# Loads of the experts' results moved into both arms of a branch, and the unused products in front of the last sums taken out

## The chip, the cores and the metric

The kernel runs on one core of one Trainium2 chip. Its time is device microseconds for one execution. The time before is 732.98 us, the median of 3 runs (732.32 to 736.02). All durations of single instructions below come from one profiled execution, which took 734.5 us.

## The reference

Two transformer layers on x of 2048 tokens by 128 features, fp32. After each of four sublayers the result is added to its input and normalised over the features (mean and variance, no gain). The first two are an attention with 16 heads and a Fourier filter; the third is a linear attention with 8 heads. The fourth is what matters here: a mixture of 8 experts, of which every token uses two.

```python
probs = softmax(flat @ router_w)                 # 2048 x 8
topw, topi = top_k(probs, 2)
combine = sum(one_hot(topi, 8) * topw[..., None], axis=1)
h = silu(einsum('td,edf->tef', flat, w1) + b1)   # 512 hidden features
y = einsum('tef,efd->ted', h, w2) + b2
out = einsum('te,ted->td', combine, y)
x = layernorm(x + res + out)                     # the last norm: the output
```

## The kernel before, in words

The tokens lie in 16 tiles of 128 rows; four tiles make a block, and there are NB = 4 blocks. The three earlier sublayers and the router take the first 625 us of the span and are not touched.

The experts work on sorted rows. The router's stage writes each token's row twice, once for each of its two experts, into the DRAM buffer `xr`, sorted by expert. A loop over pieces of BK = 256 rows then runs the experts (`experts`, L1472): `fetch_rows` loads a piece of `xr` on SyncE's queue, `copy_weights` picks the weights of its expert, `turn_rows`, `first` and `second` are the products on TensorE, and `back` (L1449) turns the piece back, scales it by the router's weight and scatters its rows by two indirect DMAs of GpSimd (L1458) into the DRAM buffer `yr`, where the first 2048 rows are the tokens' first choices and the other 2048 their second choices.

How many pieces there are depends on the data: 23 (NBK) at most. The first 19 (OFTEN) are always run. The last four are under a branch, `tc.If(many > OFTEN)` (L1504), which every engine takes for itself from a register. With the inputs used here 19 pieces suffice: the profile has 19 fetches and 38 scatters, so the other arm is the one that runs. It has no code of the kernel in it. It has only what the framework puts there: instructions that wait for the work before the branch and raise each semaphore by what the arm with four pieces would have added, so that both arms leave the same counts. The framework gives every hardware DMA one of eight semaphores in rotation, and every scatter one of eight others.

Behind the branch (L1507 to L1567) the output is made. For each block `b`:

- two loads of 256 KB fetch the first and second choices' results, `yk[0]` on SyncE's queue and `yk[1]` on ScalarE's (L1521). They read all of `yr`, so they wait for the last scatter.
- `add(b, x4s, ...)` (L1524) multiplies the residual `x4s` by the identity into the PSUM tile `zs[b]`. The 128x512 fp32 product runs as two matmul instructions.
- `sum_up(b)` (L1531) adds both `yk` to the same PSUM tile in the same way, four instructions a block.
- `stats_of` (L1535, with `stats` at L1052) has VectorE take mean and variance, `root_of` has GpSimd take the root, `shift_of` and `put` have ScalarE (for the last block VectorE too) write the normalised rows, and SyncE stores them (L1555).

Between the four residual products and the first `sum_up` stand five products of the identity with `x4s` into a tile `warm` that nothing reads (L1526 to L1529; ten instructions). From `sum_up` on, each engine keeps the order in which the kernel's text has it (`held`, L1567).

Of the kernel before, what the change touches and what calls it, by code (L numbers as in the profile page):

```python
# [9 lines left out]
F32 = mybir.dt.float32  # L10
# [8 lines left out]
P = 128  # L19
# [8 lines left out]
def tile_postln_stack(ctx: ExitStack, tc: tile.TileContext, a: dict, out: bass.AP):  # L28
    nc = tc.nc
    T, D = a["x"].shape  # L30
    NT = T // P
    TB = 4
    BW = TB * P
    NB = NT // TB
# [9 lines left out]
    NBK = 2 * T // BK + E - 1  # L44
# [13 lines left out]
    ident = const.tile([P, P], F32, name="ident")  # L58
# [77 lines left out]
    def bc(v):  # L136
        return v.unsqueeze(1).to_broadcast([P, TB, D])
# [5 lines left out]
    def slot(name):  # L143
        return banks[2].tile([P, 2, BW], F32, tag="slot", name=name)
# [18 lines left out]
    with ExitStack() as l0:  # L163
# [13 lines left out]
        warm = slot("warm")  # L177
# [405 lines left out]
        for k in range(NQ):  # L583
            b = k // 2
# [9 lines left out]
            for t in range(QT):  # L594
                i = k * QT + t
                for c in range(NP):
# [12 lines left out]
                    for heads_of, g, nt in groups:  # L609
# [3 lines left out]
                        for n, j in enumerate(heads_of):  # L613
                            for mask in (False, True)[: 1 + (g == NG - 1)]:
                                for half in range(2):
# [4 lines left out]
                                    if mask:  # L620
# [4 lines left out]
                                            start=False,  # L625
                                            stop=True,
                                        )
                                    else:
# [4 lines left out]
                                            start=True,  # L633
                                            stop=(g < NG - 1),
# [402 lines left out]
    for e in range(0, E, 2):  # L1037
        nc.sync.dma_start(
            out=wall[:, e : e + 2],
            in_=a["we"].rearrange("(e p) c -> p e c", p=P)[:, e : e + 2],  # L1040
# [8 lines left out]
    ps_a = ctx.enter_context(tc.tile_pool(name="ps_a", bufs=4, space=PSUM))  # L1049
    la = ctx.enter_context(tc.tile_pool(name="l1a", bufs=1))  # L1050
    lm = ctx.enter_context(tc.tile_pool(name="l1m", bufs=3))
# [12 lines left out]
    x4s = la.tile([P, NT, D], F32, name="x4s")  # L1064
# [261 lines left out]
    for step in SEQUENCE.split():  # L1326
        name, of = step.split(":")
# [7 lines left out]
    warm = ps.tile([P, BW], F32, tag="p", name="warm")  # L1335
    for _ in range(15):
# [4 lines left out]
            start=True,  # L1341
            stop=True,
# [30 lines left out]
    def registers(n, engine, top):  # L1373
# [10 lines left out]
    many = nc.values_load(  # L1384
        used[0:1, :],
        min_val=0,
        max_val=NBK,
        skip_runtime_bounds_check_because="so many blocks at most",
    )

    def fetch_rows(j):
        xb = lm.tile([P, KT, ROW], F32, name="xb", bufs=SOON + 2)
        nc.sync.dma_start(
            out=xb, in_=xr[bass.ds(firsts[j], BK), :].rearrange("(t p) c -> p t c", p=P)
        )
        xbs[j] = xb
# [3 lines left out]
    def copy_weights(j):  # L1400
        wt = lm.tile([P, WC], F32, name="wt", bufs=AHEAD)
        nc.vector.tensor_copy(wt, flat[:, bass.ds(offsets[j], WC)])
        wts[j] = wt

    def turn_rows(j):
        xb = xbs[j]
        pt = ps.tile([P, KT, P], F32, tag="p", name="px5")
        for t in range(KT):
            nc.tensor.transpose(pt[:, t, :], xb[:, t, 0:D], ident)
        xT = lm.tile([P, BK], F32, name="xT5")  # L1410
        nc.vector.tensor_scalar(  # L1411
            xT,
            pt.rearrange("p t d -> p (t d)"),
            cols[:, 2:3],
            cols[:, 3:4],
            ALU.mult,
            ALU.add,
        )
        xTs1[j] = xT

    def first(j):
        wt, xT = wts[j], xTs1.pop(j)
        hu = lm.tile([P, NF, BK], F32, name="hu", bufs=2)
        for f in range(0, NF, 2):
            pu = ps_a.tile([P, 2, BK], F32, tag="acc", name="pu")
            for n in range(2):
                nc.tensor.matmul(pu[:, n], wt[:, ts(f + n, P)], xT, start=True, stop=True)  # L1427
                nc.scalar.activation(  # L1428
                    hu[:, f + n],
                    pu[:, n],  # L1430
                    AF.Silu,
                    bias=wt[:, 2 * NF * P + f + n : 2 * NF * P + f + n + 1],
                )
        hus[j] = hu

    def second(j):
        wt, hu = wts.pop(j), hus.pop(j)
        acc = ps_a.tile([P, BK], F32, tag="acc", name="acc")
        for f in range(NF):
            nc.tensor.matmul(  # L1440
                acc, wt[:, ts(NF + f, P)], hu[:, f], start=(f == 0), stop=(f == NF - 1)
            )
        yT = lm.tile([P, KT, P], F32, name="yT5")
        nc.vector.tensor_scalar(
            yT.rearrange("p t d -> p (t d)"), acc, wt[:, WC - 1 : WC], None, ALU.add
        )
        yTs[j] = yT

    def back(j):  # L1449
        xb, yT = xbs.pop(j), yTs.pop(j)  # L1450
        pt = ps.tile([P, KT, P], F32, tag="p", name="py5")
        for t in range(KT):
            nc.tensor.transpose(pt[:, t, :], yT[:, t, :], ident)
        yb = lm.tile([P, KT, D], F32, name="yb")
        for t in range(KT):
            nc.vector.tensor_scalar_mul(yb[:, t], pt[:, t], xb[:, t, D + 1 : D + 2])  # L1456
        for t in range(KT):
            put = nc.gpsimd.indirect_dma_start(  # L1458
                out=yr[:, :],
                out_offset=bass.IndirectOffsetOnAxis(  # L1460
                    ap=xb.bitcast(U32)[:, t, D : D + 1], axis=0
                ),
                in_=yb[:, t, :],
                in_offset=None,
                bounds_check=2 * T - 1,
                oob_is_err=False,
            )
            tc.declare_no_dep(put.ins, group="back", reason="every row is written once")
            tc.add_to_no_dep_group("back", put.ins)
        return put  # L1470

    def experts(begin, end):  # L1472

        put = None
        for j in range(begin, min(begin + AHEAD - 1, end)):
            copy_weights(j)
        for j in range(begin, min(begin + SOON, end)):
            fetch_rows(j)
        turn_rows(begin)
        for j in range(begin, end):  # L1480
            if j + SOON < end:
                fetch_rows(j + SOON)
            first(j)
            if j + 1 < end:
                turn_rows(j + 1)
            if j > begin:
                put = back(j - 1)
            second(j)
            if j + AHEAD - 1 < end:
                copy_weights(j + AHEAD - 1)  # L1490
            if 4 <= j < 4 + NB:
                bt = ts(j - 4, TB)
                with tc.issue_after(put.ins):
                    nc.gpsimd.tensor_tensor(x3s[:, bt, :], x3s[:, bt, :], bc(mixc), ALU.subtract)
            if 4 + NB <= j < 4 + 2 * NB:
                bt = ts(j - 4 - NB, TB)
                with tc.issue_after(put.ins):
                    nc.gpsimd.tensor_tensor(x4s[:, bt, :], x3s[:, bt, :], x4s[:, bt, :], ALU.add)
        back(end - 1)


    OFTEN = NBK - E // 2
    experts(0, OFTEN)
    with tc.If(many > OFTEN, preferred_fallthrough_block=False):  # L1504
        experts(OFTEN, NBK)

    y_v = yr.rearrange("(k n p) d -> k p n d", k=2, p=P)  # L1507


    yks, zs, mvs, rs, nbs = {}, {}, {}, {}, {}  # L1510

    def add(b, src, start, stop):
        nc.tensor.matmul(  # L1513
            zs[b], ident, src.rearrange("p t d -> p (t d)"), start=start, stop=stop
        )

    for b in range(NB):
        bt = ts(b, TB)
        yk = [lm.tile([P, TB, D], F32, tag="mid", name=f"yk{k}", bufs=8) for k in range(2)]
        for k in range(2):  # L1520
            (nc.sync, nc.scalar)[k].dma_start(out=yk[k], in_=y_v[k, :, bt, :])  # L1521
        yks[b] = yk
        zs[b] = ps.tile([P, BW], F32, tag="p", name="z5")
        add(b, x4s[:, bt, :], True, False)  # L1524
    warm = ps_a.tile([P, BW], F32, tag="acc", name="warm2")
    for _ in range(5):  # L1526
        nc.tensor.matmul(  # L1527
            warm, ident, x4s[:, NT - TB :].rearrange("p t d -> p (t d)"), start=True, stop=True
        )  # L1529

    def sum_up(b):  # L1531
        for k in range(2):
            add(b, yks[b][k], False, k == 1)
# [96 lines left out]
```

## Time and profile before

| what | us |
|---|---|
| median of 3 runs | 732.98 |
| lowest, highest | 732.32, 736.02 |
| the profiled execution | 734.5 |
| its span, first to last instruction | 732.8 |
| first product of the experts (L1427) | 625.4 |
| last scatter issued (L1458) | 706.4 |
| loads of `yk` issued (L1521) | 710.6 to 712.2 |
| first statistics of the last norm (L1056) | 717.4 |
| last store issued (L1555) | 728.4 |

Of the span TensorE is busy 90%, VectorE 73%, ScalarE 64% and GpSimd 27%. These are averages over very different stages; the change is in the last 25 us. The rows of a profile name the source line, the engine, the operation and its tiles; an engine's name with a q is its sequencer, which issues DMAs and runs semaphore and branch instructions. Times are from the start of the span. The granted clock of TensorE (PEclk) is given as a share of full speed.

### The profile page before, as it was taken

What the parts mean: (1) busy time and instruction counts of PE and PEld (TensorE: products, weight loads), DVE (VectorE), ACT (ScalarE), POOL (GpSimd) and SP (SyncE); (2) the same over time, 40 slices, a digit from 0 to 9 for tenths busy, and PEclk for the clock granted to TensorE, in tenths of its full rate; (3) what the DMA queues carried; (4) which work ended last, traced back from release to release, by engine and by line L of the source; (5) the groups of instructions that cost most, each with busy time, mean ns of one, the idle gap of its engine ahead of it and who ended that gap; (6) DMA issues with size and microseconds to landing.
All of it is one profiled execution on the core that took longest, in us unless ns stands there. A gap on an engine that the chain in (4) does not pass through costs nothing. (4 is left out here: it accounts for less than half of the span.)

```text
span 732.8 us, 10664 instructions
## 1 busy us (share of the span) xinstructions
PE 660.5 (90%) x3745; PEld 374.9 (51%) x3745; DVE 531.6 (73%) x893; ACT 469.2 (64%) x1080; POOL 196.2 (27%) x203
## 2 busy tenths in 40 slices
PE   8999999999899988998899988899999818999984
PEld 7876555454345543433443333245567503788851
DVE  2566888887689897987799879887984654465514
ACT  2886988777788886876697778752554531344312
POOL 2412200220020220200500004030442786278532
PEclk9999999999999999999899999999999957999998
DMA  5802250220000214200069920050500011212115
GB/s 154 257 1 61 56 117 1 59 58 1 1 0 1 59 39 80 59 0 1 0 134 216 203 39 1 29 116 1 232 1 1 30 45 51 73 59 64 36 54 136
DMA packets 43622, 46.29 MB, mean 63 GB/s; under 512 B 3164, under 2 KB 33378, under 8 KB 43568
## 3 DMA queue, kind: packets, MB, share of 16 engines
q1 hardware_dynamic: 38896, 39.79, 23.9%
q0 software_dynamic: 2272, 4.24, 1.6%
q10 hardware_dynamic: 2400, 1.57, 0.9%
q8 instruction: 30, 0.49, 0.3%
q14 instruction: 24, 0.20, 0.1%
HBM read 23.13 MB, written 14.45 MB: 51 GB/s over the span
## 5 line engine op out<-in xcount | busy, mean ns | idle before, releaser
L647 ACT ACTIVATE sc<-sc,nmx 128x1024 f32<-128x1024 f32 (+7 forms) x384 | 321.6, 838 | 93.3 <-DVE nmx L644 65.8
L629 PE MATMUL sc<-kT,q 64*128 64x512 f32 (+7 forms) x1536 | 297.1, 508 | 19.0 <-ACT sc L647 18.0
L644 DVE TENSOR_REDUCE nmx<-sc 128x1 f32<-128x1024 f32 (+3 forms) x256 | 273.4, 1115 | 33.7 <-PE sc L629 19.6
L629 PEld LDWEIGHTS sc<-kT,q 64*128 64x128 f32 x1536 | 121.7, 187 | 143.0 <-ACT sc L647 86.8
L352 POOL TENSOR_TENSOR prod<-q,kT 128x1024 f32<-128x1024 f32 x16 | 37.5, 2350 | 195.5 <-PE pdl L364 68.0
L647 ACT ACTIVATION_READ_ACCUMULATOR sc<-sc,nmx 128x1 f32 x384 | 75.8, 197 | 0.0
L1428 ACT ACTIVATE hu<-pu,wt 128x256 f32<-128x256 f32 x76 | 33.4, 475 | 60.4 <-PE pu L1427 58.6
L104 POOL TENSOR_TENSOR ln_rs<-ln_rs,half_m 128x4 f32<-128x4 f32 x8 | 8.3, 1035 | 195.6 <-DVE ln_rs L103 195.6
L637 DVE TENSOR_REDUCE nmx<-sc 128x2 f32<-128x256 f32 (+3 forms) x64 | 51.7, 818 | 11.9 <-PE sc L621 11.3
L1458 POOL DMA_INDIRECT yr<-yb,xb x38 | 41.2, 1084 | 36.3 <-DVE yb L1456 29.3
L621 PE MATMUL sc<-rmask,lmask 64*128 64x64 bf16 x512 | 50.6, 189 | 0.0
L1427 PE MATMUL pu<-xT,wt 128*128 128x256 f32 x152 | 41.1, 393 | 0.4 <-DVE xT L1411 0.4
L621 PEld LDWEIGHTS <-lmask 64*128 64x128 bf16 x512 | 27.9, 102 | 20.8 <-issue 13.7
L1440 PE MATMUL acc<-hu,wt 128*128 128x256 f32 x152 | 35.9, 379 | 0.0
L1289 POOL DMA_INDIRECT xr<-rows,slots x32 | 31.6, 987 | 13.2 <-issue 7.9
L455 PE MATMUL pv<-x2T,pv 128*128 128x512 f32 x64 | 31.0, 612 | 2.5 <-DVE wx L461 2.1
L327 PE MATMUL pq<-x2T,pq 128*128 128x256 f32 x128 | 31.9, 392 | 1.4 <-ACT sc L647 0.9
L467 PE MATMUL py<-wx,po 128*128 128x512 f32 x64 | 31.0, 612 | 0.0
L1427 PEld LDWEIGHTS pu<-xT,wt 128*128 128x128 f32 x152 | 26.7, 189 | 8.0 <-ACT hu L1428 3.8
L1440 PEld LDWEIGHTS acc<-hu,wt 128*128 128x128 f32 x152 | 27.5, 190 | 3.2
L327 PEld LDWEIGHTS pq<-x2T,pq 128*128 128x128 f32 x128 | 23.2, 190 | 10.9 <-ACT sc L647 6.8
L461 DVE TENSOR_TENSOR wx<-pv,wx 128x1024 f32<-128x1024 f32 x16 | 19.4, 1222 | 11.4 <-DMA wx<-wd 5.9
(268 smaller groups left out, 785.4 us busy)
## 6 DMA issues: line engine op xcount, KB each, us to landing
xr<-pad SPq DMA_DIRECT2D x10, 845.0 KB, 15.4
q<-q SPq DMA_DIRECT2D x32, 256.0 KB, 3.7
wx<-wd SPq DMA_DIRECT2D x8, 1024.0 KB, 9.9
wall<-in_we_dram SPq DMA_DIRECT2D x4, 1029.0 KB, 9.5
xb<-xr SPq DMA_DIRECT2D x19, 130.0 KB, 2.3
x2T<-in_xT_dram SPq DMA_DIRECT2D x4, 256.0 KB, 5.1
xs<-in_x_dram SPq DMA_DIRECT2D x4, 256.0 KB, 6.8
yk<-yr SPq DMA_DIRECT2D x4, 256.0 KB, 5.8
```

The costliest lines, as they stand in the source:

```text
L327: nc.tensor.matmul(pm[:, n // 2, ts(n % 2, QW)], pq[:, ts(c + n, P)], x2T[:, ts(k, QW)], start=True, stop=True,)
L352: nc.gpsimd.tensor_tensor(prod, q.rearrange("p c (t e r) -> p c t e r", e=2, r=HT)[:, :, :, eo], kT[:, :, eo, ts(k, QT), :], ALU.mult,)
L621: nc.tensor.matmul(o[:, w - HT :], lmask[r, eo], rmask[r], start=False, stop=True,)
L629: nc.tensor.matmul(o, qs[k][eo][r, c, ts(t, P)], kT[r, c, eo, n0 : n0 + nt, :], start=True, stop=(g < NG - 1),)
L637: nc.vector.tensor_reduce(nm, sc.rearrange("p e (j x) -> p j e x", j=2)[:, :, :, :w], AX.XY, ALU.min,)
L644: nc.vector.tensor_reduce(nm, sc[:, :, :w], AX.XY, ALU.min)
L647: nc.scalar.activation(o, o, AF.Exp, bias=nm[:, n : n + 1], scale=-1.0, accum_out=sm[:, i % TB, 2 * c + j, g : g + 1],)
L1289: put = nc.gpsimd.indirect_dma_start(out=xr[:, :], out_offset=bass.IndirectOffsetOnAxis(ap=live["slots", u][:, k, t : t + 1], axis=0), in_ ...
L1427: nc.tensor.matmul(pu[:, n], wt[:, ts(f + n, P)], xT, start=True, stop=True)
L1428: nc.scalar.activation(hu[:, f + n], pu[:, n], AF.Silu, bias=wt[:, 2 * NF * P + f + n : 2 * NF * P + f + n + 1],)
L1440: nc.tensor.matmul(acc, wt[:, ts(NF + f, P)], hu[:, f], start=(f == 0), stop=(f == NF - 1))
L1458: put = nc.gpsimd.indirect_dma_start(out=yr[:, :], out_offset=bass.IndirectOffsetOnAxis(ap=xb.bitcast(U32)[:, t, D : D + 1], axis=0), in_= ...
```

## The change

The four pairs of loads are issued inside the branch, once in each arm: behind the four additional pieces in one, and alone in the other. Their tiles are declared ahead of the branch, so that both arms fill the same ones. The ten unused matmul instructions are taken out. The sums, the statistics and the stores stay as they are.

```diff
     experts(0, OFTEN)
-    with tc.If(many > OFTEN, preferred_fallthrough_block=False):
+    y_v = yr.rearrange("(k n p) d -> k p n d", k=2, p=P)
+    yks = {
+        b: [lm.tile([P, TB, D], F32, tag="mid", name=f"yk{k}", bufs=8) for k in range(2)]
+        for b in range(NB)
+    }
+
+    def load_results():
+        for b in range(NB):
+            for k in range(2):
+                (nc.sync, nc.scalar)[k].dma_start(out=yks[b][k], in_=y_v[k, :, ts(b, TB), :])
+
+    with tc.If(many > OFTEN, preferred_fallthrough_block=False) as more:
         experts(OFTEN, NBK)
-    y_v = yr.rearrange("(k n p) d -> k p n d", k=2, p=P)
+        load_results()
+    with more.Else():
+        load_results()
...
     for b in range(NB):
         bt = ts(b, TB)
-        yk = [lm.tile([P, TB, D], F32, tag="mid", name=f"yk{k}", bufs=8) for k in range(2)]
-        for k in range(2):
-            (nc.sync, nc.scalar)[k].dma_start(out=yk[k], in_=y_v[k, :, bt, :])
-        yks[b] = yk
         zs[b] = ps.tile([P, BW], F32, tag="p", name="z5")
         add(b, x4s[:, bt, :], True, False)
-    warm = ps_a.tile([P, BW], F32, tag="acc", name="warm2")
-    for _ in range(5):
-        nc.tensor.matmul(
-            warm, ident, x4s[:, NT - TB :].rearrange("p t d -> p (t d)"), start=True, stop=True
-        )
-
```

More of the change, by code (lines that the diff above doesn't have):

```diff
@@ L1503, in tile_postln_stack @@
     experts(0, OFTEN)
-    with tc.If(many > OFTEN, preferred_fallthrough_block=False):
+    y_v = yr.rearrange("(k n p) d -> k p n d", k=2, p=P)
[8 more added lines that the diff above has]
+    with tc.If(many > OFTEN, preferred_fallthrough_block=False) as more:
         experts(OFTEN, NBK)
-    y_v = yr.rearrange("(k n p) d -> k p n d", k=2, p=P)
-    yks, zs, mvs, rs, nbs = {}, {}, {}, {}, {}
+        load_results()
+    with more.Else():
+        load_results()
+    zs, mvs, rs, nbs = {}, {}, {}, {}
     def add(b, src, start, stop):
```

## The prediction

> **What bounds the kernel now.** Only the stage behind the branch changes, so I read first the chain of work that ended last, in order of time:
>
> ```profile
> 706.03 5.37 PE z L1513 x8
> 711.40 4.29 PE warm L1527 x10
> 715.69 1.73 PE z L1513 x4
> 717.42 0.02 issue
> 717.45 0.31 DVE ln_st L1056
> ```
>
> (Start, duration, what.) The residuals' products, the unused products and the first block's sums run without a gap; then VectorE sets the pace to the end. Its four blocks of statistics run from 717.45 to 724.95, 7.50 us. From the first statistics to the end of the span are 732.8 - 717.45 = 15.35 us. Whatever the change does must show in that first start, or in a later block's sums coming too late for VectorE (one block each 1.88 us).
>
> Next, the tile `yk`, to see what the loads allow:
>
> ```profile
> L1513 PE MATMUL z<-yk,ident x16: 592/592/592, 715.5 to 722.0; 128*128 128x512 f32 x16
> L1521 SPq DMA_DIRECT2D yk<-yr x4: 379/436/500, 710.6 to 712.2; - x4
> L1521 ACTq DMA_DIRECT2D yk<-yr x4: 472/516/517, 710.6 to 712.2; - x4
> ...
> DMA to landing us min/median/max: 3.9/6.0/8.0
> ```
>
> The trace's semaphore events put the eight landings, in order of issue (both queues by turns), at 714.52, 714.98, 716.16, 716.78, 718.00, 719.22, 719.94 and 720.26. The first sum starts at 715.53: the data was there at 714.52, and the unused products held TensorE about a microsecond longer. So loads and products both end here, nearly together.
>
> Why the loads start at 710.59 is told by the branch's own line:
>
> ```profile
> L1504 POOLq EVENT_SEMAPHORE  x4: 17/43/43, 706.6 to 708.9; - x4
> ...
> L1504 POOLq INC_SWDGE_SEM  x1: 1616/1616/1616, 709.0 to 709.0; - x1
> ```
>
> The last scatter lands at 708.81. GpSimd sees it in its arm and then takes 1.62 us to raise the scatters' semaphores for the pieces that were not run. The loads wait for that raised count (their operand in the trace is the last scatter's semaphore), and so come 1.78 us behind the landing.
>
> Last, the clock, in stretches of 3.41 us, the grid on which the trace's clock changes lie (us from and to, length, busy us of PE, PEld, DVE, ACT and POOL, then PEclk):
>
> ```profile
> core 0: us, PE busy (x) PEld busy (x) DVE busy (x) ACT busy (x) POOL busy (x), PEclk, DMA share, GB/s
> 703.12:706.53 3.41, 1.27 (x5) 0.50 (x4) 1.09 (x3) 0.00 (x0) 1.50 (x3) 1.00 0.01 3
> 706.53:709.95 3.42, 3.42 (x6) 1.33 (x5) 0.00 (x0) 0.00 (x0) 0.85 (x1) 0.50 0.11 38
> 709.95:713.36 3.41, 3.41 (x9) 1.52 (x8) 0.00 (x0) 0.00 (x0) 0.00 (x0) 1.00 0.33 79
> ```
>
> A stretch in which TensorE was busy 37% is followed by one at half clock, and a full one by full clock.
>
> **The change, part by part.**
>
> *Loads in the arm.* They now wait for the scatters themselves and not for GpSimd's count: first issue at about 708.87 for 710.59, 1.7 us earlier. Bounds: 0 if the framework lets them wait for the raised count all the same, 1.78 if nothing but the landing is left. I take 1.7, as nothing else holds SyncE or ScalarE: the trace has SyncE through the branch at 680 and ScalarE at 703. The eight issues are the same (0.4 to 0.5 us each, four on each queue) and behind them those engines have nothing before 721. GpSimd's 1.62 us stay, covered: its next work is at 719.4. The loads then land at 712.82, 713.28, 714.46, 715.08, 716.30, 717.52, 718.24, 718.56. In the arm with four pieces the loads are also there, but that arm doesn't run; it only lengthens a jump that took 0.44 us on ScalarE (702.90 to 703.34) and 0.36 on TensorE; I cost that at nothing for ScalarE, hidden by its wait till 708.8, and at 0 to 0.4 us for TensorE, whose code in the arm does not grow: 0.
>
> *Unused products out.* Ten instructions 0.43 us apart, 4.29 us, all of it in the chain. TensorE is then free at 711.40 and waits for data. What it gains depends on what it waits for and on the clock it then has.
>
> *A new wait that the diff doesn't show.* Each arm now has its own load of the same tile, and they need not carry the same semaphore. In the trace the loads carry 116, 117, 118, 100, 101, 102, 103, 104 in order, beginning right behind the last fetch's 104, although the four fetches of the other arm stand between them in the text; so the rotation begins anew from the same place in each arm. In the long arm the four fetches take 116, 117, 118, 100, and its loads begin at 101, four places on. A reader behind the branch that must be safe on both paths waits for the semaphore of either arm's load. For the first block in the arm that runs, that is 116 and 101: its own landing and that of the load four places on. So block 0's first sum waits for block 2's first load, the second for block 2's second; block 1 waits for block 3 in the same way; blocks 2 and 3 wait for counts that the arm itself raises on SyncE once the first four loads have landed (715.1), earlier than their own data. Queued behind the waiting sum on TensorE are only the other sums; VectorE waits for them.
>
> With this wait: TensorE idles from 711.40 to 716.30. Its 4.9 us hold at least one whole stretch below half busy, so it starts at half clock, where the timeline has L1513 0.853 us from one instruction to the next (706.54, 707.39, 708.24) and 1.06 us for one. Block 0's four start at 716.34, 717.19, 718.05 (its data is there at 717.52) and 718.90, and end at 719.95. First statistics 719.99 for 717.45: +2.54. The stretch to 720.19 is full, so the clock is back then; block 1 is summed by 721.9, 0.14 late for VectorE. Sum +2.7 us. The grid lies elsewhere in other runs: the half clock lasts 3.4 to 6.8 us from 716.3, and the worst gives 8 instructions at 0.853, block 1 at 723.4, and +4.1.
>
> *The Trainium skill on the clock.* "TensorE: Matmul & The Clock Gate" (Part 1: The HAM clock gate) has the clock fall after an idle stretch of about 3.4 us, and advises no gap over about 3 us. The trace is stricter: 1.79 busy us of 3.42 (52%, at 348.13) were followed by half clock, 1.98 of 3.41 (58%, at 283.28) were not. For the wait above rule and rows agree. Without it the gap is 711.40 to 712.85, 1.45 us: by the rule harmless, by the rows at the very edge (58% busy at worst). And a plain removal of the unused products with loads at the old time would leave 3.1 us: by the rule at its limit, by the rows half clock.
>
> **The rivals.**
>
> *A: each sum waits for its own load alone* (the framework rotates alike in both arms, or keeps the arms apart). Sums start at 712.85; four at 0.43 apart end at 714.73; statistics 714.77, which is -2.68. Block 2's second load at 717.52 costs 0.13. Time 734.5 - 2.55 = 731.95, not slower than before. It decides if the first sum starts before about 715. For it: the landings. Against it: the rotation read above. If the clock is lost in that gap, block 0 ends at 712.85 + 3 x 0.853 + 1.06 = 716.47, and A gives about 733.6.
>
> *C: the loads come no earlier*, since they wait for GpSimd's count in the arm too. Then the sums start at 714.55 with half clock, end at 718.17, and the first statistics are 0.75 late: 735.3. For it: the framework waits broadly elsewhere (GpSimd waits for all eight scatter semaphores). Against it: the count is raised for the pieces that weren't run, and a load inside the arm need not know of them.
>
> *The expected case, B,* is the cross wait.
>
> **How the numbers follow.** The profiled execution took 734.5 us, 1.7 around its span, and stands 1.5 above the median of 732.98. Part of that may be the half clock at 706.53: at full clock the residuals and unused products would end at 713.9, the sums wait for the load of 714.98, and the statistics begin at 716.08, 1.37 earlier. Case B doesn't profit from that, as it starts at 716.34 either way. So B is 734.5 + 2.7 = 737.2 if the 1.5 is the clock, and 732.98 + 2.7 = 735.7 if all runs share this tail; up to 1.4 more by the grid. I take 736.6, own range 735.3 to 738.6.
>
> Chances: B 0.62, A 0.26, C 0.07, something else (code fetched at the longer branch, say) 0.05. A measurement of this kernel can tell about 0.5% (3.7 us) from no change, so the bounds are 729.3 and 736.65. B is cut by the upper one: 0.36 slower, 0.26 the same. A gives 0.23 the same and 0.03 faster, C 0.07 the same, the rest 0.04 slower and 0.01 faster. Together: faster 0.04, same 0.56, slower 0.40. The range 731.5 to 738.6 takes in B and most of A.
>
> **What would show it.** Loads of `yk` at about 708.9 show the first step right. B: TensorE idle from 711.4 to about 716.3, ended by the landing of a load of block 2; instructions 0.85 us apart; PEclk 0.5 from about 713 to 720; first statistics near 720. A: first sum near 712.9, statistics near 714.8. C: loads still at 710.6. I would be wrong altogether if the sums wait for all eight loads (statistics after 721) or if an engine stalls at the branch.

## The result, and the profile after

The changed kernel is slower: 741.46 us median of 7 runs (737.80 to 743.59), beside 732.98 for the kernel before (7 runs, 732.32 to 738.07). The ratio of the two, from all of these runs, is 1.0072 with a 95% interval of 1.0049 to 1.0095; it is not the quotient of the two medians, which is 1.0116. Repeated later beside 45 runs of the kernel before it was 739.41 to 735.71, ratio 1.0044 (1.0027 to 1.0061). The profiled execution took 739.21 us, its span 737.5, for 734.5 and 732.8 before.

The chain of work that ended last now goes through a load (start, duration, what):

```profile
710.33 0.43 SPq L1514
...
710.86 6.68 DMA yk<-yr
...
717.58 6.36 PE z L1527 x8
```

The unused products are gone from it, but so is the start of the sums at 715.7. The load of 710.86 is the third on SyncE's queue, which belongs to block 2, and behind it eight instructions take 6.36 us where before four took 1.73. The tile `yk` tells what TensorE waited for:

```profile
L1527 PE MATMUL z<-yk,ident x16: 592/593/1222, 717.6 to 726.8; 128*128 128x512 f32 x16
L1514 SPq DMA_DIRECT2D yk<-yr x4: 377/440/453, 709.8 to 711.4; - x4
...
  DMA yk<-yr: 15.1, 3
```

The kernel before had this in the last line's place:

```profile
  DMA yk<-yr: 0.2, 1
```

Loads are issued at 709.83, and the sums wait for them 15.1 us in total (TensorE's products and its weight loads are counted apart). In the trace's semaphore events block 0's own loads land at 713.83 and 714.31; block 2's land at 717.54 and 718.38. The first sum starts at 717.58, 0.04 behind the first of block 2's, and the second sum's weights are loaded at 718.60, also behind block 2's. The first weight load waits for semaphore 101 (block 2's first load), and the wait ahead of it was for 116 (its own).

The branch's line shows the load's side:

```profile
L1516 POOLq EVENT_SEMAPHORE  x4: 17/43/43, 707.6 to 709.9; - x4
...
L1516 POOLq INC_SWDGE_SEM  x1: 1616/1616/1616, 710.0 to 710.0; - x1
```

GpSimd's 1.62 us are still there, but the loads are issued before they begin, 0.02 us behind the last scatter's landing at 709.82.

The clock (from and to, length, busy us of PE, PEld, DVE, ACT, POOL, then PEclk):

```profile
705.88:709.29 3.41, 2.24 (x6) 1.07 (x7) 0.23 (x1) 0.00 (x0) 1.95 (x2) 1.00 0.11 38
709.29:712.71 3.42, 1.44 (x4) 0.37 (x2) 0.00 (x0) 0.00 (x0) 0.00 (x0) 1.00 0.31 90
712.71:716.12 3.41, 0.00 (x0) 0.00 (x0) 0.00 (x0) 0.00 (x0) 0.00 (x0) 1.00 1.18 313
716.12:719.53 3.41, 1.95 (x3) 0.92 (x4) 0.00 (x0) 0.00 (x0) 0.00 (x0) 0.50 0.90 215
719.53:722.94 3.41, 3.41 (x6) 1.35 (x5) 1.40 (x8) 0.00 (x0) 0.00 (x0) 0.50 0.00 0
```

TensorE does nothing in the third stretch and has half clock in the next two, just when the sums come. One thing differs by chance: the residuals' products fell into the first two stretches and kept full clock here. They end at 710.73, 0.91 us behind the last scatter's landing; in the profile before they had half clock and ended 2.59 us behind it.

Of the 4.7 us by which the span is longer, 1.0 lies ahead of the branch, where the program is the same: the last scatter lands at 709.82 for 708.81. Over all profiles of this study it landed between 707.40 and 711.23. The earliest of them had 30.7 us of half clock ahead of the experts' last product, the others 37.6 to 44.4. So I compare from here on the tail, from that landing to the end of the span: 732.79 - 708.81 = 23.98 us before and 737.49 - 709.82 = 27.67 after. The other 3.7 us are taken as the change's.

### The profile page after: what moved, and what is told of

Read it like the earlier page. It is cut to its first block, busy times and chain, and to the rows that moved or that the text cites. A ratio compares the mean times of both kernels' runs of the same rounds, so it can differ in the third digit from the quotient of the medians.

```text
span 737.5 us, 10648 instructions
## 1 busy us (share of the span) xinstructions
PE 657.3 (89%) x3735; PEld 373.3 (51%) x3735; DVE 531.8 (72%) x893; ACT 469.2 (64%) x1080; POOL 196.4 (27%) x203
## 5 line engine op out<-in xcount | busy, mean ns | idle before, releaser
L1440 PE MATMUL acc<-hu,wt 128*128 128x256 f32 x152 | 35.9, 379 | 0.0
L1440 PEld LDWEIGHTS acc<-hu,wt 128*128 128x128 f32 x152 | 27.5, 190 | 3.2
```

The source lines that it names most:

```text
L1440: nc.tensor.matmul(acc, wt[:, ts(NF + f, P)], hu[:, f], start=(f == 0), stop=(f == NF - 1))
```

## The experiments

The theory is the prediction's: a sum waits for its own load and for the one that carries its semaphore in the other arm, and in that wait TensorE loses its clock. The rivals are that the clock alone did it, or that the arms cost something in themselves. The tails come from one profile each; the ratios to the kernel before come from all runs (spare_two has only four).

| kernel | places apart | unused instructions | first sum after landing, us | first statistics, us | tail, us | ratio (95%) |
|---|---|---|---|---|---|---|
| before | - (loads behind the branch) | 10 | 6.72 | 8.64 | 24.0 | 1 |
| changed | 4 | 0 | 7.77 | 11.59 | 27.7 | 1.0072 (1.0049 to 1.0095) |
| changed, again | 4 | 0 | 7.84 | 11.56 | 26.9 | 1.0044 (1.0027 to 1.0061) |
| arms_products | 4 | 10 | 7.37 | 9.95 | 25.3 | 1.0020 (1.0006 to 1.0035) |
| behind_noproducts | - (behind) | 0 | 5.81 | 9.63 | 25.1 | 1.0021 (0.9999 to 1.0042) |
| matched | 0 | 0 | 3.94 | 5.96 | 21.5 | 0.9981 (0.9965 to 0.9998) |
| matched, again | 0 | 0 | 4.07 | 6.09 | 21.5 | 0.9989 (0.9972 to 1.0006) |
| matched_products | 0 | 10 | 7.06 | 8.98 | 24.3 | 1.0009 (0.9989 to 1.0029) |
| matched_two | 0 | 4 | 4.66 | 6.58 | 21.9 | 0.9970 (0.9954 to 0.9986) |
| matched_into_z | 0 | 4 | 4.25 | 6.27 | 21.6 | 0.9980 (0.9963 to 0.9997) |
| spare_six | 2 | 0 | 5.77 | 9.56 | 25.8 | 1.0008 (0.9985 to 1.0032) |
| spare_two | 6 | 0 | 9.78 | 13.60 | 29.3 | 1.0085 (1.0053 to 1.0117) |

**One half at a time.** All diffs but that of behind_noproducts are against the changed kernel. The first keeps the unused products:

```diff
         add(b, x4s[:, bt, :], True, False)
+    warm = ps_a.tile([P, BW], F32, tag="acc", name="warm2")
+    for _ in range(5):
+        nc.tensor.matmul(
+            warm, ident, x4s[:, NT - TB :].rearrange("p t d -> p (t d)"), start=True, stop=True
+        )
```

> The change without its second half: loads in both arms, the ten unused product instructions kept. Theory (each sum waits for two loads, the other one four places on, and TensorE loses its clock in that wait): the first sums still wait for block 2's loads, about 7.7 and 8.6 us behind the last scatter's landing, but TensorE comes to them at full clock, so the first statistics start about 9.6 us behind that landing (8.6 in the kernel before, 11.6 in the changed one) and block 1 is not late. Some 1 us slower than before, some 2.7 us faster than the changed kernel. Rival (the clock alone: the unused products were what kept TensorE fast, and the waits don't matter): no slower than before, 0 to 1 us faster. Rival (the arms themselves cost, by jumps or code): as slow as the changed kernel.

Measured: ratio 1.0020, tail 25.3 us, first statistics 9.95 behind the landing (9.6 expected; the second sum had to wait once more, till 719.34, for block 2's second load). The sums are still late, as the theory has it, but they run at full clock:

```profile
L1527 PE MATMUL z<-yk,ident x16: 592/592/697, 717.9 to 725.0; 128*128 128x512 f32 x16
```

The middle and the longest instruction are 592 and 697 ns, for 593 and 1222 in the changed kernel. The tail is 27.7 - 25.3 = 2.4 us shorter than the changed kernel's, and 1.6 shorter than in its repetition (below). Of that, 0.4 to 0.5 is not the clock: the awaited load landed that much earlier here (first sum at 7.37 for 7.77 and 7.84). So with the cross wait in place the lost clock is worth 1 to 2 us. That the kernel is slower than before at full clock tells against the rival of the clock alone.

The second takes only the unused products out of the kernel before (its diff is against that one):

```diff
-    warm = ps_a.tile([P, BW], F32, tag="acc", name="warm2")
-    for _ in range(5):
-        nc.tensor.matmul(
-            warm, ident, x4s[:, NT - TB :].rearrange("p t d -> p (t d)"), start=True, stop=True
-        )
```

> The other half alone: loads behind the branch as before, unused products taken out. Theory: the sums start with the first loads (5.7 us behind the last scatter's landing) after an idle of about 3 us, mostly at half clock; first statistics about 9.4 us behind the landing for 8.6 before: 0.5 to 1.5 us slower than before. Rival (the clock alone): nearly all of the loss of the changed kernel, 3 to 5 us slower than before. Rival (the arms cost): as before.

Measured: ratio 1.0021, tail 25.1, first statistics at 9.63. The sums come 0.9 us earlier than before and the statistics 1.0 later:

```profile
709.91:713.33 3.42, 1.17 (x3) 0.19 (x1) 0.00 (x0) 0.00 (x0) 0.00 (x0) 1.00 0.01 4
713.33:716.74 3.41, 0.64 (x1) 0.50 (x2) 0.00 (x0) 0.00 (x0) 0.00 (x0) 0.50 0.92 252
```

A stretch with TensorE busy 1.17 of 3.42 us (34%), then half clock. TensorE was idle for 5.0 us, not the 3 expected, as the residuals' products had full clock in this profile and ended early. Neither half alone costs what both do: 1.3 and 1.1 us of tail, 2.4 in sum, against 3.7 and, repeated, 2.9 together.

**The rotation.** Here only the arm that doesn't run is edited. Its four additional loads fill a tile that nothing reads:

```diff
         experts(OFTEN, NBK)
+        for n in range(4):
+            spare = lm.tile([P, E], F32, name="spare", bufs=4)
+            nc.sync.dma_start(out=spare, in_=a["rw"])
         load_results()
```

> The changed kernel with four small loads of a table (spare, nothing reads them) ahead of the results' loads in the arm that does not run, so that the rotation of the semaphores stands at the same place in both arms; nothing that executes is added but four more raised counts. Theory: every sum then waits for its own load alone; the first sum starts about 4.1 us behind the last scatter's landing instead of 7.7, the first statistics 6 us behind it if the clock holds and 7.7 if it does not (11.6 in the changed kernel, 8.6 before): 3 to 6 us faster than the changed kernel and 0.5 to 2.5 us faster than before. Both rivals (clock alone; arms cost): the same as the changed kernel, as TensorE has the same gap and the arms stay.

Measured: ratio 0.9981, tail 21.5. The spare loads are never executed, yet the sums start 3.94 us behind the landing for 7.77. Each now waits for its own load; in the trace the weight loads of the first four pairs wait for 116, 117, 118 and 100, the semaphores that these loads carry:

```profile
L1530 PE MATMUL z<-yk,ident x16: 592/592/697, 711.3 to 718.3; 128*128 128x512 f32 x16
L1514 SPq DMA_DIRECT2D yk<-yr x4: 376/376/428, 707.4 to 709.1; - x4
```

From the first load at 707.4 to the first sum at 711.3 it is 3.9 us. TensorE's gap in front of it is 1.95 us, for 6.86 in the changed kernel, and did not cost the clock:

```profile
707.81:711.22 3.41, 1.58 (x4) 0.38 (x2) 0.00 (x0) 0.00 (x0) 0.00 (x0) 1.00 0.64 190
711.22:714.63 3.41, 3.29 (x8) 1.42 (x8) 1.17 (x7) 0.00 (x0) 0.00 (x0) 1.00 1.21 296
```

The rival that the arms cost falls, as they are in this kernel too. So does the one of the clock alone: it had this kernel as slow as the changed one. The spare tile and the longer arm do not explain the gain either, since the kernels with two and with six spare loads (below) have them as well, and their first sums come late.

> The matched rotation with the ten unused product instructions put back. Theory: the sums start when the unused products end or the first loads land, whichever is later: 4.1 to 6.7 us behind the last scatter's landing at full clock, so the first statistics 7 to 8.6 us behind it: 0 to 1.5 us faster than before. The rival that the arms cost: 3 us or more slower than before. The rival of the clock alone: no different from before.

Its diff is the spare loads and the ten unused instructions together. Measured: ratio 1.0009, tail 24.3, first statistics at 8.98. That misses the theory's numbers (7 to 8.6 us, faster than before) by 0.4 us at the upper end:

```profile
711.63 4.56 PE L1540 MATMUL warm<-x4s,ident 128*128 128x512 f32 x10 [0.40 <-ACTq L1516]
```

The bracket has the idle time before these instructions and what ended it: the unused products begin 0.40 us late, for a reason that the version with two products shows below. With that, and with the residuals at half clock, they hold TensorE until the first sum at 7.06, long after the data is there, and give back all that the earlier loads gained. The rival that the arms cost, at 3 us or more, is refuted all the same.

**The distance.** With two spare loads the arms stand six places apart, with six they stand two apart:

> Two spare loads in place of four in the arm that does not run: the rotation stands six places apart, so block 0's sums wait for block 3's loads. Theory: first sum about 9.6 us behind the last scatter's landing (7.8 in the changed kernel), first statistics 13.1 to 13.4 (11.6), tail 28.5 to 29.5 us: 1 to 2 us slower than the changed kernel. Rival (any pair of arms with unlike semaphores costs the same, whichever load it is): as the changed kernel, 27 to 28 us.

> Six spare loads in place of four: two places apart, so block 0's sums wait for block 1's loads (5.7 and 6.3 us behind the last scatter's landing) and block 1's for block 2's. Theory: first sum about 5.8 us, at half clock; first statistics 8.4 to 9.6, tail 24 to 26 us, between the matched rotation (21.5) and the changed kernel (27.7), about as before. Rival (any unlike pair costs the same): 27 to 28 us.

Measured: tails of 29.3 and 25.8. The first sums start at 9.78 and 5.77 us, where block 3's first load (9.74) and block 1's (5.63) land. The chain of the kernel with two spare loads:

```profile
712.21 8.14 DMA yk<-yr
720.35 0.04 issue
720.40 5.93 PE z L1530 x8
```

So it is not a fixed price for unlike arms: the wait is for the very load that has the semaphore, and its place sets the price. The statistics at two spare loads came at 13.60, 0.2 beyond what was expected; those at six at 9.56, inside.

**The change again.**

> The changed kernel once more, beside the same runs of the kernel before as the next ones, because runs of one kernel differ by up to 6 us with the places at which the clock falls earlier on. Theory: tail from the last scatter's landing to the end 27 to 29 us (24.0 before), so 3.0 to 5.0 us slower than before (ratio 1.004 to 1.007). Rival (something ahead of the branch, such as the place of code or buffers, has become slower too): 6 us or more slower, with a tail of 28 us at most.

Measured: tail 26.9, just under the theory's 27, and ratio 1.0044, at its lower end. The first comparison's 1.0072 has an interval that overlaps it. A cost ahead of the branch is not needed to explain the ratio, but two comparisons whose middles differ by 0.3% mark how finely the runs tell.

**A version that beats both.** With the matched rotation, two products (four instructions) in place of five:

> The matched rotation with two unused products (four instructions) in place of five: they end about when the first loads land, so that no idle stretch is left in which the clock falls, and hold up nothing. Theory: first sum 3.9 to 4.1 us behind the last scatter's landing, first statistics about 6, tail 21.5 us in every run: 2.5 us faster than before (ratio 0.996 to 0.998) and 0 to 1 us faster than the matched rotation without products, whose clock falls in some runs. Rival (the short tail of the matched profile was a lucky place of the clock): tail 23 to 24 us, no faster than before.

Measured: ratio 0.9970, tail 21.9, the sums 0.6 us later than expected. The profile shows why, in the bracket behind the unused products:

```profile
706.77 5.37 PE L1530 MATMUL z<-x4s,ident 128*128 128x512 f32 x8 [1.56 <-PEq L1516]
713.06 1.98 PE L1540 MATMUL warm<-x4s,ident 128*128 128x512 f32 x4 [0.92 <-ACTq L1516]
```

They waited 0.92 us for ScalarE's branch line. Their PSUM tile was last read by ScalarE in the other arm, and ScalarE raises that count in this arm only behind its four loads. A tile that needs no such count:

```diff
         zs[b] = ps.tile([P, BW], F32, tag="p", name="z5")
+        for n in range(2 if b == NB - 1 else 0):
+            add(b, x4s[:, bt, :], True, True)
         add(b, x4s[:, bt, :], True, False)
```

> The matched rotation with two unused products that go into the last block's PSUM tile ahead of its residual (which starts the tile anew), so that they need no tile which ScalarE has read. In the run with two products into a tile of their own those began 1.1 us late, since they waited for a count that ScalarE's arm raises only behind its four loads. Theory (the raised count held them): no gap now between the residuals' products and the unused ones; first sum 3.9 to 4.6 us behind the last scatter's landing, first statistics 6.0 to 6.6, tail 21.5 to 22.1 us; ratio to the kernel before 0.996 to 0.998. Rival (TensorE paused for another reason there, its code or the clock): the gap of about 1 us stays.

```profile
705.68 7.08 PE L1530 MATMUL z<-x4s,ident 128*128 128x512 f32 x12 [1.56 <-PEq L1516]
713.38 2.84 PE L1530 MATMUL z<-yk,ident 128*128 128x512 f32 x6 [0.61 <-DMA yk<-yr]
```

Measured: the twelve instructions run as one, tail 21.6, ratio 0.9980.

> The matched rotation without unused products once more, on the chip and beside the runs of the one with two products. Theory: tail 21.5 us where the clock holds in the gap before the first sum, 23 to 24 where it falls; ratio to the kernel before 0.996 to 0.999, 0 to 1 us slower than with two products.

Measured: tail 21.5, ratio 0.9989. The three matched versions with none or two products overlap in their intervals; matched_two and matched_into_z are faster than the kernel before (0.3% and 0.2%), and whether the few products are worth anything beside none is open.

**What the tails leave out.** The tail starts at the last scatter's landing, and that landing is not the same in all kernels. In every profile the scatter is issued 3.3 us behind the start of the experts' last product (L1440). It lands 5.73 to 5.87 us behind that start in the five profiles without spare loads, but 5.90 to 6.41 behind it in the seven with them. Counted from that product, the two matched profiles are 1.9 and 2.1 us shorter than the kernel before, not 2.5. The traces suggest why: in each of them one packet of 16 KB of instructions is moved at the same time. It ends 1.16 to 1.87 us behind the scatter's issue, and the scatter lands 1.15 to 1.23 us behind that end. No run here moves that packet alone, so this is argued, not shown.

## Why the prediction was right or wrong

The direction and the mechanism were right; the size in absolute time was not.

- *Loads in the arm, 1.7 us earlier.* Right: issued 0.02 us behind the last scatter's landing for 1.78, so 1.76.
- *Jump and arm at nothing.* Right for the changed kernel: from the start of the experts' last product to the first of the residuals' products it is 2.96 us before and 2.98 after, and to the last scatter's landing 5.73 and 5.74. With spare loads in the arm the landing is up to 0.7 later.
- *The new wait.* Right in every place: block 0 waited for block 2, and moving the rotation by edits that don't run moved the first sum to block 1, block 3 or its own load. Forecast were 7.5 us from the landing to the first sum (716.34 - 708.81), measured 7.77.
- *Half clock during the first block.* Right: first statistics 11.2 forecast, 11.59 measured. The idle time was forecast as 4.9 us; it was 6.86 in this profile, whose residuals had full clock, and 5.3 in the repetition, where they had half clock as before. The lateness of block 1 was taken as 0.14; it was 0.7 in this profile, as the second half-clock stretch lasted to 722.94, and nothing in the repetition, where it ended earlier. The tail grew by 3.7 and 2.9 for a forecast of 2.7 to 4.1.
- *The number itself.* 736.6 was too low, and 741.46 lies above the range as it stands; measured as a ratio (1.0072 of 732.98 is 738.3) it lies inside. Over the kernel before, the forecast was 3.6 us or 0.5%, and measured were 0.7 and, repeated, 0.4%. A change too small to tell had been held likelier (0.56) than a slower kernel (0.40); both intervals lie above 1. The mis-sized term is the base. I held the profile to stand 1.5 above a typical run and took the result down from 737.2. Over the later comparisons the kernel before has medians of 735.56 to 735.83, so 734.5 was no high value, and 732.98 a low one. From 735.7 the forecast's 2.7 to 4.1 us give 738.4 to 739.8, and the repetition's median is 739.41. The other 2 us of 741.46 lie within the spread of the seven runs.
- *The clock's edge.* Wrong, without harm to the expected case: from the stretch at 348.13 (52% busy, then half clock) I held a stretch under about half busy to be enough. In the changed kernel 1.44 of 3.42 us (42%) kept full clock, in matched 1.58 of 3.41 (46%). That made case A look riskier than it was. The rule of the Trainium skill ("TensorE: Matmul & The Clock Gate", Part 1: The HAM clock gate), an idle stretch of about 3.4 us, fits the changed kernel's empty one, but in behind_noproducts a stretch with 1.17 of 3.42 us busy (34%) brought half clock too. (The advice on gaps of 3 us stands further down that page, under "Why this matters for your kernels".)
- *Case A.* Its tail was worked out as 24.0 - 2.55 = 21.4; matched has 21.5. The case was right as arithmetic and described another program.
- *Case C.* Loads did not wait for GpSimd's count. Its arithmetic for loads at the old time (0.75 late) comes near what behind_noproducts measures: 1.0.
- *The estimate of 1.37 us* for runs of the kernel before whose clock does not fall at the branch. Too large: four sums 0.43 us apart from 714.55 on end at 716.43, so the statistics would begin at 716.46, 1.0 earlier.

What stays open: the ratios of the two matched comparisons are 0.9981 and 0.9989. Shorter by 1.9 to 2.1 us, as counted from the experts' last product, would be 0.997; that lies inside the first interval and at the edge of the second. If the kernel before has runs whose clock does not fall at the branch, their earlier statistics would close part of the rest, but no profile here shows such a run.

## What to carry to other kernels

A load that is issued in both arms of a branch is, for its reader, two loads: count the DMAs ahead of it in each arm, and if the two places in the rotation differ, the reader waits for a stranger (2, 4 and 6 places of the eight were tried here). Evening them out in the arm that doesn't run turned a loss of 0.4 to 0.7% into a gain of 0.1 to 0.2%, the smaller one within the noise; the last scatter landed 0.4 to 0.6 us later with it. A time counted from an event near the change can hide such a shift, so count from an earlier one too. And unused products are priced by the wait that they fill: ten instructions hid the old wait, were too many for the shorter one, and for the longer one saved 1 to 2 us by the clock.

## What the runs showed of the hardware that I had not expected

The profile's busy share of TensorE alone does not tell what its clock does next. Among the stretches at the branch, those of 34, 37 and 39% (behind_noproducts, before, spare_six) were followed by half clock, and those of 42, 46 and 50% (changed, matched, matched again) by full clock. But in the attention a stretch of 52%, with products of 64 rows and of 128 columns, was followed by half clock (at 348.13 in the kernel before). What makes the difference was not tested. And GpSimd's one instruction that raises the scatters' semaphores takes 1.62 us, which stood unseen between a landing and the loads that waited for it.
